# Layer-1 attention, near tiles: keeping the sums made for the maxima instead of making the product a second time

## The chip, the cores and the metric

The kernel runs on one core of a Trainium2 chip. The metric is the device time of one execution in microseconds, lower is better. Before the change the median of three runs is 1308.65 us (1305.66 to 1311.44).

## The reference

Two transformer-like layers over x of shape (2, 1024, 128). Each layer normalises x and adds to it an attention and a mixture-of-experts feed-forward block, both computed from the same normalised rows. Layer 0 has a causal sigmoid attention; layer 1 has a softmax attention with a relative position term, and only that one is touched here. Its core, for each of 16 heads of width 8:

```
q, k, v = heads(x @ Wq.T), heads(x @ Wk.T), heads(x @ Wv.T)
att_rel_pos = einsum('bhsd,pd->bhsp', q, pos_emb_k)           # pos_emb_k: 256 positions
att_idxs = clip(ar[None, :] - ar[:, None], -128, 127) % 256   # key index minus query index
att_pos = att_rel_pos[:, :, ar[:, None], att_idxs]
attn_val = einsum('bhqd,bhkd->bhqk', q, k)
att = softmax((attn_val + att_pos) / sqrt(8), axis=-1)
y = einsum('bhqk,bhkd->bhqd', att, v) ... @ Wproj.T
```

Because the index is clipped at 128, the position term of a pair of 128-row tiles varies from element to element only where query tile and key tile are the same or neighbours. Everywhere else it is one constant per query row.

## The kernel before, in words

The 1024 rows of a batch are 8 tiles of 128. Heads are handled four at a time: the 16 heads are split in four sets `s`, and in a set each of the four heads sits in its own group `r` of 32 partitions (`rows_of(r)`), so that TensorE can work on four heads side by side. A *group* `n` of work is one batch `b`, one set `s` and one half `q` of the queries (four query tiles, `i` = 0 to 3); there are 16 groups. Each group takes 8 *steps*, one for each key tile `kt`, so there are 128 steps `t`, with the key tile on the partitions and 512 queries along the columns.

For a group, in order of time:

- `by_position` makes the position scores of two query tiles at a time and writes them to a bounce buffer in HBM. `near_by` reads them back skewed, so that each query row is shifted by its own index. The result is the tile `near[n, i]`, of 128 queries x 4 heads x 384 columns: the position scores (less the far constant) of the three key tiles around query tile `i`. It lies in one of ten slots.
- `scan(n, i, half)` runs LEAD = 10 steps ahead of the step that uses it, one half of the keys each step. It makes the scores with the queries on the partitions (L902), and VectorE takes the row maxima: `tensor_reduce` (L927) where the position term is constant, and a sum-and-maximum (L922) where it isn't, which adds `near` to the scores, writes the sums to a scratch tile `junk`, and keeps only their maximum. After the second half L930 puts the negated maximum into a spare column of `negmax`.
- `augment` turns the negated maxima and adds them to the queries as an extra row of the contraction (`qa`), two steps ahead of the group's first step. So a product with `qa` comes out less the maximum. The far constants are in the keys in the same manner: `kls` for keys up to and with the near range, `khs` for keys above it.
- `scores(n, kt)` fills four PSUM banks, one for each head `r`. For query tiles near `kt` it turns the block of `near` into the bank (L953, with an identity), and then adds the product of keys and `qa` for all four query tiles to it (L963). ScalarE takes the exponential of each bank (L970).
- `values(n, kt, part)` multiplies the exponentials with the values (L982); it runs one step after its scores. `unload`, `finish` and `project` end a group or a half.

The banks come from one rotation of seven (`small()`). A step takes four for its scores and four for its scan, so that the fourth bank of the next step's scores is the first bank of this step's scan.

The order of TensorE's instructions is the program's order (`manual_schedule`); in each step it is: scores, values of the step before, scan, and then what stands beside. On the other engines a scheduler chooses the order of the instructions when the kernel is built; on the chip each engine then follows its own list. In the second batch GpSimd (POOL in the profile) also serves the mixture of experts: `gather(i)` fetches 128 rows by index (L630), and `gathered(i)` scales them (L640) and adds them to the result (L641). There are 64 of these, from step 68 on, placed three in four steps apart. `operands` makes `kls`, `khs` and `vs` on POOL too (L834, L837), once for each set, seven steps ahead of their first scan. Between step 66 and step 67 TensorE computes the experts (L704, L719). In the first batch POOL issues 64 scatters (L618), two each step from step 33 on, each held until the exponentials of its step (`paced`).

Of the kernel before, what the change touches and what calls it, by code (L numbers as in the profile page):

```python
# [10 lines left out]
F32 = mybir.dt.float32  # L11
AF = mybir.ActivationFunctionType
ALU = mybir.AluOpType
# [4 lines left out]
P = 128  # L18
# [3 lines left out]
NT = T // P  # L22
# [5 lines left out]
NG = 4  # L28
EPS = 1e-5
BIG = 3.0e38  # L30
# [11 lines left out]
NEAR = 3 * P  # L42
# [4 lines left out]
def fused_layers_kernel(ctx: ExitStack, tc: tile.TileContext, a: dict, out: bass.AP):  # L47
# [11 lines left out]
    nc = tc.nc  # L59
# [22 lines left out]
    def small():  # L82
        if "sm" not in psum:
            return big()[:, 0, :]
        return psum["sm"].tile([P, TB], F32, tag="sm", name="sm")
# [10 lines left out]
    def load(pool, name, shape, src=None):  # L96
        t = pool.tile(shape, F32, tag=name, name=name, bufs=1)
        nc.sync.dma_start(t, a[name] if src is None else src)
        return t
# [12 lines left out]
    w1 = load(l0, "w1", [P, E0 * I0])  # L112
# [656 lines left out]
    full, head, near, qa, negmax, yacc, probs = {}, {}, {}, {}, {}, {}, {}  # L769
# [23 lines left out]
    def four_banks():  # L793
        if "sm" in psum:
            return [small() for _ in range(NG)]
        pairs = [big(), big()]
        return [pairs[r // 2][:, r % 2, :] for r in range(NG)]

    def rows_of(r):
        return slice(32 * r, 32 * r + 32)  # L800
# [83 lines left out]
    def spans(lo, hi, cut):  # L884

        c = min(max(lo, cut), hi)
        return [(lo, c, 0)] * (lo < c) + [(c, hi, 1)] * (c < hi)
# [3 lines left out]
    def scan(n, i, half):  # L891

        b, s, q = groups[n]
        l1 = pools["l1"]
        qs, kl, kh, _ = head[b, s]
        qt = 4 * q + i
        ps = four_banks()
        lo, hi = 4 * half, 4 * half + 4
        for k0, k1, far in spans(lo, hi, qt + 2):
            for r in range(NG):  # L900
                g = rows_of(r)
                nc.tensor.matmul(  # L902
                    ps[r][:, (k0 - lo) * P:(k1 - lo) * P], qs[g, qt * P:(qt + 1) * P],
                    (kh if far else kl)[g, k0 * P:k1 * P], start=True, stop=True,
                )
        if half == 0:
            maxima[n, i] = l1.tile([P, NG, 4], F32, tag="maxima", name="maxima", bufs=3), []
        mx, used = maxima[n, i]
        n0, n1 = max(lo, qt - 1), min(hi, qt + 2)
        if n0 >= n1:  # L910
            pieces = [(lo, hi, False)]
        else:
            pieces = [(lo, n0, False)] * (lo < n0) + [(n0, n1, True)] + [(n1, hi, False)] * (n1 < hi)
        for k0, k1, close in pieces:
            slot = len(used)
            used.append(slot)
            for r in range(NG):
                part = ps[r][:, (k0 - lo) * P:(k1 - lo) * P]
                if close:
                    junk = l1.tile([P, NEAR], F32, tag="junk", name="junk")  # L920
                    w0 = (k0 - (qt - 1)) * P
                    nc.vector.tensor_tensor_reduce(  # L922
                        junk[:, 0:(k1 - k0) * P], part, near[n, i][:, r, w0:w0 + (k1 - k0) * P],
                        1.0, -BIG, ALU.add, ALU.max, mx[:, r, slot:slot + 1],
                    )
                else:
                    nc.vector.tensor_reduce(mx[:, r, slot:slot + 1], part, AX.X, ALU.max)  # L927
        if half == 1:
            out_ = negmax[s, i].rearrange("p (r c) -> p r c", r=NG)[:, :, aux[s]]
            nc.vector.tensor_reduce(out_, mx[:, :, 0:len(used)], AX.X, ALU.max, negate=True)  # L930

    def augment(n):

        b, s, q = groups[n]
        ps = small()
        for i in range(4):
            nc.tensor.matmul(
                ps[:, i * P:(i + 1) * P], negmax[s, i], ident, is_transpose=True, start=True, stop=True
            )
        t = pools["l1"].tile([P, TB], F32, tag="qa", name="qa", bufs=2)  # L940
        nc.vector.tensor_add(t, head[b, s][0][:, q * TB:(q + 1) * TB], ps)
        qa[n] = t

    def scores(n, kt):

        b, s, q = groups[n]
        _, kl, kh, _ = head[b, s]
        ps = [small() for _ in range(NG)]
        close = [i for i in range(4) if abs(4 * q + i - kt) <= 1]
        for r in range(NG):  # L950
            for i in close:
                w0 = (kt - (4 * q + i) + 1) * P
                nc.tensor.matmul(  # L953
                    ps[r][:, i * P:(i + 1) * P], near[n, i][:, r, w0:w0 + P], ident,
                    is_transpose=True, start=(i == close[0]), stop=False, skip_group_check=True,
                )

        cut = min(max(kt - 1 - 4 * q, 0), 4)
        parts = [(0, cut, kh)] * (cut > 0) + [(cut, 4, kl)] * (cut < 4)
        for m, (i0, i1, k) in enumerate(parts):  # L960
            for r in range(NG):
                g = rows_of(r)
                nc.tensor.matmul(  # L963
                    ps[r][:, i0 * P:i1 * P], k[g, kt * P:(kt + 1) * P], qa[n][g, i0 * P:i1 * P],
                    start=(m == 0 and not close), stop=(m == len(parts) - 1), skip_group_check=True,
                )
        p = pools["late"].tile([P, NG * TB], F32, tag="p", name="p", bufs=2)
        p = p.rearrange("p (r c) -> p r c", r=NG)
        for r in range(NG):
            e = nc.scalar.activation(p[:, r, :], ps[r], AF.Exp)  # L970
        last_exp["name"] = e.ins.name
        probs[n, kt] = p
# [129 lines left out]
    for m in range(LEAD):  # L1102
        at(N_ATT + 8 + m, scan, m // 8, m % 8 // 2, m % 2)
# [83 lines left out]
    with tc.manual_schedule(engines={mybir.EngineType.PE}):  # L1187
        near_by(1, 1)
        for t in range(N_STEPS + 1):
# [7 lines left out]
            if t < N_STEPS:  # L1197
                scores(t // 8, t % 8)


            n, kt = (t - 1) // 8, (t - 1) % 8
# [3 lines left out]
            m = t + LEAD  # L1205
            if m < N_STEPS:
                scan(m // 8, m % 8 // 2, m % 2)
# [9 lines left out]
            n, k = (t - 9) // 8, (t - 9) % 8  # L1217
            if t >= 9 and k == 0:
                unload(n)
            b, s, q = groups[min(max(n, 0), len(groups) - 1)]  # L1220
# [64 lines left out]
```

## Time and profile before

| | before |
|---|---|
| median of 3 runs | 1308.65 us |
| the profiled execution | 1308.08 us |
| its span | 1306.3 us |
| TensorE busy | 1197.7 us (92%) |
| VectorE busy | 759.4 us (58%) |
| ScalarE busy | 625.0 us (48%) |
| GpSimd busy | 378.2 us (29%) |
| steps of layer-1 attention, first batch | about 520 to 880 us |
| experts | about 880 to 1010 us |
| steps of layer-1 attention, second batch | about 1010 to 1306 us |

How to read it. The profile is of one execution. A row of the groups names a source line, the engine, the operation, what it writes and reads, and how often; then the busy time and the mean of one in ns; then how long the engine stood idle just before and who ended that. A matmul of fp32 operands is recorded as two, so the 704 transposes are 704 records, and the four products of a step eight. PEld is the loading of weights and overlaps PE. POOL's time that it stands waiting for a transfer isn't counted as busy. A timeline row has the start, the duration, the engine and the line, and in brackets the idle time of the engine ahead of it. Times that are not starts or durations of one instruction are in microseconds from the start of the span.

### The profile page before, as it was taken

What the parts mean: (1) busy time and instruction counts of PE and PEld (TensorE: products, weight loads), DVE (VectorE), ACT (ScalarE), POOL (GpSimd) and SP (SyncE); (2) the same over time, 40 slices, a digit from 0 to 9 for tenths busy, and PEclk for the clock granted to TensorE, in tenths of its full rate; (3) what the DMA queues carried; (4) which work ended last, traced back from release to release, by engine and by line L of the source; (5) the groups of instructions that cost most, each with busy time, mean ns of one, the idle gap of its engine ahead of it and who ended that gap; (6) DMA issues with size and microseconds to landing.
All of it is one profiled execution on the core that took longest, in us unless ns stands there. A gap on an engine that the chain in (4) does not pass through costs nothing.

```text
span 1306.3 us, 23125 instructions
## 1 busy us (share of the span) xinstructions
PE 1197.7 (92%) x8567; PEld 566.9 (43%) x8567; DVE 759.4 (58%) x2178; ACT 625.0 (48%) x1102; POOL 378.2 (29%) x464
## 2 busy tenths in 40 slices
PE   5889999989999878899799999988999999998997
PEld 2323332333333333434344354448999444443433
DVE  7783333573322358776876756764555856666653
ACT  3634444535455342454355654543444555554463
POOL 1123243323323242001002444330000445446453
PEclk9889999989999989899899999998999999998998
DMA  6682212111111261344365644659997354663511
GB/s 181 175 229 85 59 57 57 33 33 49 41 49 41 82 217 61 126 147 145 98 194 178 201 142 161 218 185 278 293 293 228 110 171 157 208 215 115 181 47 29
DMA packets 146660, 181.77 MB, mean 139 GB/s; under 512 B 16436, under 2 KB 125236, under 8 KB 146292
## 3 DMA queue, kind: packets, MB, share of 16 engines
q1 hardware_dynamic: 142292, 171.37, 42.7%
q0 software_dynamic: 4256, 8.92, 2.4%
q8 instruction: 68, 1.11, 0.4%
q14 instruction: 44, 0.36, 0.1%
HBM read 110.81 MB, written 73.77 MB: 141 GB/s over the span
## 4 chain that ended last, share of the span: by engine, by line
PE 70%; DVE 17%; DMA 5%; ACT 4%; issue 2%; POOL 1%; SPq 0%; DVEq 0%; ACTq 0%; POOLq 0%
PE sm L963 11%; PE sm L902 9%; PE acc L982 8%; PE big L340 6%; PE sm L953 5%; PE big L449 5%; PE big L341 5%; PE acc L475 5%; PE ffn L367 4%; PE sm L704 4%; DVE junk L922 3%; PE sm L853 3%; DVE maxima L927 2%; PE sm L719 2%; DMA room<-wx 1%
## 5 line engine op out<-in xcount | busy, mean ns | idle before, releaser
L970 ACT ACTIVATE p<-sm 128x512 f32<-128x512 f32 x512 | 264.7, 607 | 234.1 <-PE sm L963 233.6
L927 DVE TENSOR_REDUCE maxima<-sm 128x1 f32<-128x512 f32 (+3 forms) x472 | 226.7, 502 | 99.2 <-PE sm L902 99.2
L455 ACT ACTIVATE at<-big 128x1024 f32<-128x1024 f32 (+1 forms) x192 | 144.9, 808 | 149.7 <-PE big L449 143.7
L922 DVE CUSTOM_DVE_ANT_0 junk<-sm,near 128x384 f32<-128x384 f32 (+2 forms) x292 | 130.3, 446 | 66.3 <-PE sm L902 66.3
L982 PE MATMUL acc<-p,vs 128*32 128x512 f32 (+1 forms) x1288 | 146.4, 524 | 0.4 <-ACT yu L994 0.4
L352 DVE SCALAR_TENSOR_TENSOR t<-big,b,sg 128x512 f32<-128x512 f32 x64 | 47.9, 749 | 158.0 <-ACT sg L351 158.0
L355 POOL TENSOR_TENSOR h<-h,cb 128x512 f32<-128x512 f32 x64 | 82.8, 1294 | 195.5 <-DVE h L353 185.3
L953 PE MATMUL sm<-ident,near 128*128 128x128 f32 x704 | 108.4, 287 | 24.5 <-DVE maxima L927 11.3
L902 PE MATMUL sm<-kls,qs 32*128 32x512 f32 (+2 forms) x776 | 107.5, 580 | 6.2 <-POOL kls L834 5.0
L963 PE MATMUL sm<-qa,kls 32*128 32x512 f32 (+3 forms) x832 | 112.9, 560 | 0.0
L630 POOL DMA_INDIRECT got<-slots_y,slot_of x64 | 65.1, 1017 | 164.6 <-ACT p L970 152.5
L953 PEld LDWEIGHTS sm<-ident,near 128*128 128x128 f32 x704 | 78.0, 143 | 79.2 <-ACT p L970 35.4
L449 PE MATMUL big<-qm,xT 32*128 32x512 f32 (+3 forms) x768 | 103.8, 555 | 1.3 <-DVE xT L249 0.6
L618 POOL DMA_INDIRECT slots_x<-xn,slot_of x64 | 62.8, 981 | 95.8 <-ACT p L970 86.3
L475 PE MATMUL acc<-at,xn 128*32 128x512 f32 (+3 forms) x768 | 84.8, 514 | 5.9 <-POOL at L460 4.0
L340 PE MATMUL big<-xT,w 128*128 128x512 f32 x128 | 74.5, 665 | 14.9 <-DVE h L353 12.5
L857 ACT COPY rel<-sm 128x512 f32<-128x512 f32 x112 | 57.5, 600 | 61.6 <-PE sm L853 61.6
L640 POOL TENSOR_SCALAR got<-got,share 128x128 f32<-128x128 f32 x64 | 41.1, 642 | 110.1 <-DMA got<-slots_y,slot_of 110.0
L367 PE MATMUL ffn<-h,w 128*128 128x512 f32 x128 | 72.8, 651 | 0.0
L982 PEld LDWEIGHTS acc<-p,vs 128*32 128x32 f32 x1288 | 26.6, 109 | 105.9 <-issue 95.4
L902 PEld LDWEIGHTS sm<-kls,qs 32*128 32x128 f32 x776 | 36.9, 186 | 81.1 <-ACT p L970 21.1
L460 POOL TENSOR_SCALAR_AFFINE_SELECT at<-at 128x512 f32<-128x512 f32 x64 | 41.5, 648 | 101.6 <-ACT at L455 101.2
(285 smaller groups left out, 1659.8 us busy)
## 6 DMA issues: line engine op xcount, KB each, us to landing
bounce<-rel SPq DMA_DIRECT2D x64, 768.0 KB
near<-bounce SPq DMA_DIRECT2D x64, 768.0 KB
cb<-cw SPq DMA_DIRECT2D x128, 128.0 KB
blockw<-wx SPq DMA_DIRECT2D x53, 304.0 KB
room<-wx SPq DMA_DIRECT2D x26, 304.0 KB
slots_x<-zeros SPq DMA_DIRECT2D x19, 256.0 KB
slots_y<-by SPq DMA_DIRECT2D x19, 256.0 KB
room<-slots_x SPq DMA_DIRECT2D x17, 256.0 KB
```

Source lines behind the costliest of these rows:

```text
L340: nc.tensor.matmul(hh[0:m, 0, :], wa, xT, start=True, stop=True)
L367: nc.tensor.matmul(y, w2m, h[0:m], start=first, stop=last and bias_mm is None)
L449: nc.tensor.matmul(halves[r // 2][:, r % 2, off:TB], xT0[b][g, kt * P:(kt + 1) * P], masked[b, s][g, q * TB + off:(q + 1) * TB], start=Tru ...
L455: nc.scalar.activation(at[:, 2 * j:2 * j + 2, off:TB], sc[:, :, off:TB], AF.Sigmoid, scale=4.0 / math.sqrt(HD))
L475: nc.tensor.matmul(y[32 * r:32 * r + 32, off:TB], xn0[b][:, kt * P + 32 * r:kt * P + 32 * r + 32], at[:, r, off:TB], start=(kt == 0), stop ...
L902: nc.tensor.matmul(ps[r][:, (k0 - lo) * P:(k1 - lo) * P], qs[g, qt * P:(qt + 1) * P], (kh if far else kl)[g, k0 * P:k1 * P], start=True, s ...
L922: nc.vector.tensor_tensor_reduce(junk[:, 0:(k1 - k0) * P], part, near[n, i][:, r, w0:w0 + (k1 - k0) * P], 1.0, -BIG, ALU.add, ALU.max, mx[ ...
L927: nc.vector.tensor_reduce(mx[:, r, slot:slot + 1], part, AX.X, ALU.max)
L953: nc.tensor.matmul(ps[r][:, i * P:(i + 1) * P], near[n, i][:, r, w0:w0 + P], ident, is_transpose=True, start=(i == close[0]), stop=False, ...
L963: nc.tensor.matmul(ps[r][:, i0 * P:i1 * P], k[g, kt * P:(kt + 1) * P], qa[n][g, i0 * P:i1 * P], start=(m == 0 and not close), stop=(m == l ...
L970: e = nc.scalar.activation(p[:, r, :], ps[r], AF.Exp)
L982: nc.tensor.matmul(y[rows_of(r), part], vs[:, kt, rows_of(r)], probs[n, kt][:, r, part], start=(kt == 0), stop=(kt == NT - 1 and part.stop ...
```

## The change

The sums of scores and position scores that the scan makes for near tiles are kept in place, in `near` itself, and `junk` is gone. After the maximum of a query tile is known, its negation is added to the kept sums of the four heads: head 0 on ScalarE, head 1 on VectorE, heads 2 and 3 on GpSimd. The block that `scores` turns into the bank is then complete. The product with `qa` is left out for the near query tiles, and runs only over the query tiles ahead of them (with `khs`) and behind them (with `kls`). The loop over the transposes now has the query tile outside and the head inside, and each block is a group of its own in the bank.

```diff
                 if close:
-                    junk = l1.tile([P, NEAR], F32, tag="junk", name="junk")
+
                     w0 = (k0 - (qt - 1)) * P
+                    whole_ = near[n, i][:, r, w0:w0 + (k1 - k0) * P]
                     nc.vector.tensor_tensor_reduce(
-                        junk[:, 0:(k1 - k0) * P], part, near[n, i][:, r, w0:w0 + (k1 - k0) * P],
-                        1.0, -BIG, ALU.add, ALU.max, mx[:, r, slot:slot + 1],
+                        whole_, part, whole_, 1.0, -BIG, ALU.add, ALU.max, mx[:, r, slot:slot + 1],
                     )
...
             nc.vector.tensor_reduce(out_, mx[:, :, 0:len(used)], AX.X, ALU.max, negate=True)
+            w0, w1 = (max(qt - 1, 0) - (qt - 1)) * P, (min(qt + 2, NT) - (qt - 1)) * P
+            for r in range(NG):
+                t = near[n, i][:, r, w0:w1]
+                if r == 0:
+                    nc.scalar.activation(t, t, AF.Identity, bias=out_[:, r:r + 1])
+                else:
+                    (nc.vector if r == 1 else nc.gpsimd).tensor_scalar(t, t, out_[:, r:r + 1], None, ALU.add)
...
-        close = [i for i in range(4) if abs(4 * q + i - kt) <= 1]
-        for r in range(NG):
-            for i in close:
-                w0 = (kt - (4 * q + i) + 1) * P
+        c0, c1 = (min(max(kt + d - 4 * q, 0), 4) for d in (-1, 2))
+        for i in range(c0, c1):
+            w0 = (kt - (4 * q + i) + 1) * P
+            for r in range(NG):
                 nc.tensor.matmul(
                     ps[r][:, i * P:(i + 1) * P], near[n, i][:, r, w0:w0 + P], ident,
-                    is_transpose=True, start=(i == close[0]), stop=False, skip_group_check=True,
+                    is_transpose=True, start=True, stop=True,
                 )
-        cut = min(max(kt - 1 - 4 * q, 0), 4)
-        parts = [(0, cut, kh)] * (cut > 0) + [(cut, 4, kl)] * (cut < 4)
-        for m, (i0, i1, k) in enumerate(parts):
+        for i0, i1, k in ((0, c0, kh), (c1, 4, kl)):
             for r in range(NG):
-                g = rows_of(r)
-                nc.tensor.matmul(
-                    ps[r][:, i0 * P:i1 * P], k[g, kt * P:(kt + 1) * P], qa[n][g, i0 * P:i1 * P],
-                    start=(m == 0 and not close), stop=(m == len(parts) - 1), skip_group_check=True,
-                )
+                if i0 < i1:
+                    g = rows_of(r)
+                    nc.tensor.matmul(
+                        ps[r][:, i0 * P:i1 * P], k[g, kt * P:(kt + 1) * P], qa[n][g, i0 * P:i1 * P],
+                        start=True, stop=True,
+                    )
```

In the profile of the changed kernel the sum-and-maximum is L923, the subtraction on ScalarE is L935, those on VectorE and GpSimd are L937, the transposes are L960, the products L969 and the exponentials L976; L927, L930 and the gathers' L630, L640 and L641 keep their numbers.

## The prediction

> **What bounds the kernel now.** I read first the page's busy shares and its chain, then TensorE's timeline over one near group, then POOL's timeline over the last third, and last what the tile of the gathered rows waits for.
>
> ```profile
> PE 1197.7 (92%) x8567; PEld 566.9 (43%) x8567; DVE 759.4 (58%) x2178; ACT 625.0 (48%) x1102; POOL 378.2 (29%) x464
> PE 70%; DVE 17%; DMA 5%; ACT 4%; issue 2%; POOL 1%; SPq 0%; DVEq 0%; ACTq 0%; POOLq 0%
> L953 PE MATMUL sm<-ident,near 128*128 128x128 f32 x704 | 108.4, 287 | 24.5 <-DVE maxima L927 11.3
> L963 PE MATMUL sm<-qa,kls 32*128 32x512 f32 (+3 forms) x832 | 112.9, 560 | 0.0
> ```
>
> TensorE is bound on average, and POOL at 29% looks free. Averages hide stages, so next TensorE's timeline in attention of layer 1 (start, duration, engine, line, form, count, idle before):
>
> ```profile
> 668.95 1.14 PE L902 MATMUL sm<-kls,qs 32*128 32x512 f32 x8
> 670.02 0.55 PE L953 MATMUL sm<-ident,near 128*128 128x128 f32 x3
> 671.02 0.30 PE L953 MATMUL sm<-ident,near 128*128 128x128 f32 x1 [0.45 <-DVE maxima L922]
> 671.25 1.14 PE L963 MATMUL sm<-qa,kls 32*128 32x512 f32 x8
> ...
> 674.39 1.27 PE L953 MATMUL sm<-ident,near 128*128 128x128 f32 x8
> 675.59 1.14 PE L963 MATMUL sm<-qa,kls 32*128 32x512 f32 x8
> 676.66 1.07 PE L982 MATMUL acc<-p,vs 128*32 128x512 f32 x8
> ...
> 678.73 1.53 PE L953 MATMUL sm<-ident,near 128*128 128x128 f32 x12
> 680.19 1.14 PE L963 MATMUL sm<-qa,kls 32*128 32x512 f32 x8
> ```
>
> Twelve transposes take 1.46 us start to start, 0.122 each; a full product L963 takes 1.07, so 0.268 per 128 columns. The fourth head group (r=3) cannot start until DVE has emptied a bank of the scan before it: with four transposes TensorE stops after three and resumes 1.00 us after it began. With twelve, r=3 comes after nine and nothing stops.
>
> Now POOL near the end, with TensorE's line at the same time:
>
> ```profile
> 1179.97 1.01 POOL L630 DMA_INDIRECT got<-slots_y,slot_of  x1 [0.15 <-issue]
> 1182.67 0.60 POOL L640 TENSOR_SCALAR got<-got,share 128x128 f32<-128x128 f32 x1 [1.68 <-DMA got<-slots_y,slot_of]
> 1183.35 0.45 POOL L641 TENSOR_TENSOR x<-x,got 128x128 f32<-128x128 f32 x1
> 1183.80 1.19 POOL L834 TENSOR_SCALAR khs<-kf,not_aux,k_add 128x1024 f32<-128x1024 f32 x1
> 1184.98 1.19 POOL L834 TENSOR_SCALAR kls<-kf,not_aux,k_add 128x1024 f32<-128x1024 f32 x1
> 1186.22 1.45 PE L902 MATMUL sm<-kls,qs 32*128 32x256 f32 x8 [5.03 <-POOL kls L834]
> 1294.86 0.61 POOL L641 TENSOR_TENSOR x<-x,got 128x128 f32<-128x128 f32 x1
> ```
>
> This is the reading that matters. POOL issues a gather, waits for it, scales it, adds it, then issues the next. All 64 run from 1020.25 to 1295.47: 275.2 us, 4.30 each, of which only 136.3 are busy and 110.0 are waits for the DMA. They are placed at 0.75 step each; a step of TensorE here is about 4.4 us, so it allows 3.3. POOL is busy half the time and yet **late**, by more each step: keys placed seven steps ahead already cost TensorE 5 us at 1186. Nothing else urgent stood in that queue.
>
> **What the Trainium skill says.** "PSUM — Partial Sum Buffer", Engine vs sequencer instructions: the queues of ScalarE, VectorE and GpSimd are strictly first in, first out. The trace agrees: the key operands at 1183.80 sat behind the gathers. "DMA: Bandwidth & Descriptors", Anatomy of one DMA: a transfer issued by GpSimd has a fixed cost of about 2 us, mostly the receipt; here the median from issue to landing is 2.7. "GPSIMD Engine Reference", Elementwise: 512 elements of one input took 769 ns; this trace's 128x512 select (L460) took 648 and I use the trace. "SBUF — State Buffer", Who interferes with whom: a VectorE instruction in a two-port mode blocks GpSimd wholly. L640 has 0.60 us as median and 1.30 as maximum, so blocking may be there; I use it for the upper price only.
>
> **The change part by part.**
>
> Removed: the second product for near blocks. Of 32 blocks (8 key tiles x 4 query tiles) in a group 11 are near; 16 x 11 x 0.268 = 47 us of TensorE, if nothing else came up. The transposes stay, 704.
>
> Moved: the transposes now run with r innermost, so r=3 is always fourth. By the 1.00 us above, twelve take 1.00 + 9 x 0.122 = 2.10 (was 1.46), eight 1.61 (was 1.20), four stay 1.23. Two groups (q=0 and 1) have 4, 4 and 2 such steps: 4 x 0.64 + 4 x 0.41 = 4.2 us back of 11 x 2 x 0.268 = 5.9. The compiled order of DVE also changes: for the second query tile, four sums L923 now come ahead of the four other reductions. That frees the first bank 3 x 0.47 = 1.4 us later, once ahead of a twelve-transpose step and once ahead of a step without near blocks. Net for two groups -1.7 + 1.4 to 2.8, so between -0.3 and +1.1. For the 8 groups ahead of the gathers -1 to +4; with a good day for the overlaps -15, with ACT's waits below +8. I take **0**.
>
> The sum kept instead of junk: same instruction, same size, same engine; the write goes to SBUF as before. Nothing, and no transfer is delayed, since a near slot is refilled only after its transposes anyway.
>
> Added on DVE: 64 subtractions of up to 384 columns. L234 (128 columns) 0.34, L824 (1024) 0.79: about 0.47, one in two steps. DVE idles over 1 us in a near step (58% busy); hidden, else 64 x 0.47 = 30 us. On ACT: 64 of 384 columns, 0.48 as the 384-column copies L696; ACT idles 1.4 to 2.9 us a step. It stands among the exponentials and waits for the maximum; behind it are two or three exponentials that free banks and feed L982. That is in the +8.
>
> Added on POOL: 128 subtractions, r=2 and 3. Not in the trace as such. L640 has 0.60 at 128 columns, L834 1.19 at 1024: 0.66 ns a column, so 0.77 at 384 and 0.68 at 256, plus 0.08 between instructions. A quarter have 256 columns: 0.83 each. Flat bound 0.68; upper bound 1.08 (blocked by VectorE, or the slope of a two-input add). Below nothing is excluded: the work is new. Until the gathers POOL waits for exponentials of the same step, and the tiles are needed five steps or more later: hidden. In the compiled queue 25 pairs stand among the gathers, each between one row's addition and the next gather, so the DMA waits do not cover them; the last two pairs stand behind all 64 gathers. Queued behind them: all later gathers. Waiting for them: TensorE's transposes, five to twelve steps after the scan. SP's queue gains nothing.
>
> Sum, for the last group's tile i=2, needed in step 125:
> - first gather 1020.3 + 0; gathers 275.2; 50 subtractions x 0.83 = 41.4; fewer waits for the DMA, as the same near and bounce traffic spreads over 15% more time: waits above their floor of 57 (each four gathers: 0.3 + 1.63 + 1.63) are 53, of which 13% is 7. POOL ends at 1329.9.
> - tail: step 125's third tile started at 1281.3 of 1306.3, so 25.0 remain, less 2.1 for narrower products, less 1.4 as the very last pair is needed later: 21.5. Span 1351.4.
> - plus 1308.1 - 1306.3 = 1.8: **1353 us**, against the profiled execution's 1308.1, +45; the median of the runs, 1308.65, is 0.6 higher, within my rounding.
>
> TensorE first stops at step 82: tile i=3 of group 10 stands behind 14 gathers and seven pairs (60 + 13 us) and is wanted after 14 x 4.4 = 62. From there it follows POOL.
>
> **The rivals.** *POOL keeps up (faster).* If TensorE stayed the bound, the result is 1308 less 8 x 1.7 = 14: about 1294. For it: 110 us of POOL's stage are waits. Against: even at no price the subtractions behind the gathers are ready at 1295, and step 125 wants them at 1281. The stage must shrink by 14 + 41 = 55 us, more than all 53 of avoidable waits. *Only TensorE's new stalls.* If POOL were somehow in time, but the bank waits and ACT's place in the queue cost the upper figure: 1308 + 8 x 1.1 = 1317. It decides if r=3's bank is freed later than 1.7 us after the transposes begin. *Worse than the sum.* POOL blocked by VectorE at 1.08 each, the waits not fewer, and the groups ahead of the gathers at +8: 1353 + 13 + 7 + 8 = 1381; beyond, if each stop of TensorE also lowers its granted clock (0.87 in the stretch with the 5 us stop).
>
> **How the numbers follow.** POOL's queue 0.83; POOL in time 0.08, of which most faster; only the stalls 0.04; worse 0.05. The unknowns of the first give 1353 - 7 (flat price) - 13 (more of the waits gone) - 15 = 1318, and 1381 upward. Range 1318 to 1381, about 8 in 10. A measurement of this kernel can tell about 0.5%, 6.5 us, from no change. Faster 0.07, same 0.04, slower 0.89.
>
> **What would show it.** Right: the transposes (L960 then) waiting tens of us for POOL's subtraction (L937) after 1080; POOL's last instruction a subtraction near 1330, about 21 us ahead of the end; the products (L969) shorter by some 40 us busy; TensorE idle from about 1080 on, little change at 1020. Wrong: gathers under 3.5 us each, POOL ending by 1285, the transposes waiting mostly for ACT or DVE, or the first gather moved by over 15 us.

## The result, and the profile after

The changed kernel takes 1418.96 us, median of 4 runs (1400.51 to 1421.84), against 1309.36 us for the kernel before, median of 4 runs. The ratio is 1.0793, 95% interval 1.0686 to 1.0901. (The ratio compares the means of the fast runs: the run at 1421.84, over 1.5% above the fastest, counts as slow and is left out, so it isn't the quotient of the medians.) The profiled execution took 1416.86 us, its span 1415.1 us: 63.7 us more than the 1351.4 of the prediction's sum.

The page of the changed kernel, first the same rows as before: busy shares, the chain, the transposes and the largest row of the products; then the two new rows of subtractions, on ScalarE and GpSimd.

```profile
PE 1238.5 (88%) x8247; PEld 573.3 (41%) x8247; DVE 782.3 (55%) x2242; ACT 656.5 (46%) x1166; POOL 536.4 (38%) x592
PE 54%; DVE 20%; DMA 10%; ACT 6%; POOL 5%; issue 5%; SPq 0%; DVEq 0%; ACTq 0%; POOLq 0%
L937 POOL TENSOR_SCALAR near<-near,negmax 128x384 f32<-128x384 f32 (+1 forms) x128 | 156.7, 1232 | 307.8 <-DVE negmax L930 235.1
L960 PE MATMUL sm<-ident,near 128*128 128x128 f32 x704 | 125.2, 308 | 69.9 <-POOL near L937 38.9
L935 ACT ACTIVATE near<-near,negmax 128x384 f32<-128x384 f32 (+1 forms) x64 | 37.7, 589 | 168.0 <-DVE negmax L930 109.8
L969 PE MATMUL sm<-qa,kls 32*128 32x512 f32 (+3 forms) x512 | 84.1, 524 | 4.9 <-DVE maxima L927 3.2
```

TensorE's share of the chain fell from 70% to 54%; DMA, POOL, VectorE, ScalarE and issue took it. TensorE issues 320 records less and yet is recorded as busy for longer: a longer busy time doesn't mean more work here (the last section has the lower granted clock of this run). The row to look at is L937: 1.232 us for one, where the prediction's sum had 0.77 and 0.68 for the two sizes. Kept apart by shape it reads:

```profile
L937 POOL TENSOR_SCALAR near<-near,negmax 128x384 f32<-128x384 f32 x96 | 126.4, 1325 | 268.1 <-DVE negmax L930 210.2 <-issue 26.4 <-DVE chosen L274 17.3
L937 POOL TENSOR_SCALAR near<-near,negmax 128x256 f32<-128x256 f32 x32 | 30.3, 954 | 39.7 <-DVE negmax L930 24.9 <-issue 14.8
```

The waits of the changed kernel from 500 us to the end (who <- for whom: us in total, times, longest):

```profile
POOL got L640 <- DMA got<-slots_y,slot_of: 108.8, 49, 6.7
ACT near L935 <- DVE negmax L930: 106.0, 34, 6.7
PEld sm L960 <- POOL near L937: 43.4, 15, 13.1
PE sm L960 <- POOL near L937: 38.9, 12, 12.9
```

The last two rows are the same stops seen by the weight loads and by the matmuls, so TensorE stood some 40 us for POOL's subtraction. The first row is the DMA wait of the gathers, 108.8 against 110.0 before: the gathers wait as they did. And ScalarE stood in front of its own subtraction for 106 us. Whether these waits of ScalarE cost anything is a question for the experiments.

POOL's timeline towards the end, and TensorE's at the same time:

```profile
1335.11 1.02 POOL L630 DMA_INDIRECT got<-slots_y,slot_of  x1 [0.15 <-issue]
...
1340.47 2.47 POOL L937 TENSOR_SCALAR near<-near,negmax 128x384 f32<-128x384 f32 x2
1343.11 1.04 POOL L630 DMA_INDIRECT got<-slots_y,slot_of  x1 [0.16 <-issue]
1345.76 0.61 POOL L640 TENSOR_SCALAR got<-got,share 128x128 f32<-128x128 f32 x1 [1.62 <-DMA got<-slots_y,slot_of]
...
1387.42 4.28 POOL L937 TENSOR_SCALAR near<-near,negmax 128x384 f32<-128x384 f32 x4
```

```profile
1336.43 1.83 PE L960 MATMUL sm<-ident,near 128*128 128x128 f32 x10
1341.78 0.48 PE L960 MATMUL sm<-ident,near 128*128 128x128 f32 x1 [3.51 <-POOL near L937]
1343.00 0.48 PE L960 MATMUL sm<-ident,near 128*128 128x128 f32 x1 [0.75 <-POOL near L937]
```

Ten of twelve transposes run, then heads 2 and 3 wait until POOL has made their subtractions at 1340.47, and those stand between an addition and the next gather. The last two pairs, at 1387.42, stand behind all 64 gathers. Since POOL's last instruction ends at 1391.70, the span divides into three parts:

| us | prediction's sum | measured | more |
|---|---|---|---|
| start to first gather | 1020.3 | 1059.1 | 38.8 |
| first gather to end of POOL | 309.6 | 332.6 | 23.0 |
| end of POOL to end | 21.5 | 23.4 | 1.9 |

More than half of what was missed lies ahead of the gathers, where POOL's subtractions were taken to be hidden and the rest to cost 0. There the layer-1 steps of the first batch, from the first near transpose to the experts' first instruction, take 397.8 us against 362.7 before; 4.0 of the 38.8 lie ahead of that stretch and the experts are 0.3 shorter. One place in it, read on three engines: ScalarE, then TensorE, then the one instruction of VectorE that both wait for.

```profile
649.06 2.06 ACT L976 ACTIVATE p<-sm 128x512 f32<-128x512 f32 x4 [2.16 <-PE sm L969]
655.11 0.61 ACT L935 ACTIVATE near<-near,negmax 128x384 f32<-128x384 f32 x1 [3.98 <-DVE negmax L930]
655.63 2.04 ACT L976 ACTIVATE p<-sm 128x512 f32<-128x512 f32 x4
```

```profile
651.09 0.55 PE L960 MATMUL sm<-ident,near 128*128 128x128 f32 x3
652.92 0.30 PE L960 MATMUL sm<-ident,near 128*128 128x128 f32 x1 [1.28 <-DVE maxima L923]
653.15 0.93 PE L969 MATMUL sm<-qa,khs 32*128 32x384 f32 x8
654.58 1.46 PE L902 MATMUL sm<-kls,qs 32*128 32x512 f32 x6
656.26 1.12 PE L902 MATMUL sm<-kls,qs 32*128 32x512 f32 x2 [0.22 <-ACT p L976]
```

```profile
654.90 0.17 DVE L930 TENSOR_REDUCE negmax<-maxima 128x4 f32<-128x12 f32 x1
```

ScalarE is done with four exponentials at 651.12 and stands 3.98 us in front of its subtraction, whose maximum VectorE makes in the instruction at 654.90. The next four exponentials are behind it in the queue, although TensorE's products for them are under way from 653.15. They start at 655.63, and the scan's last matmuls (656.26) wait for a bank that the first of them empties. The same lines show the other stop: the fourth transpose waits 1.28 us for a bank that VectorE empties.

### The profile page after: what moved, and what is told of

It reads as the page before. It is cut to its first block, busy times and chain, and to the rows that moved or that the text cites. A ratio compares the mean times of both kernels' runs of the same rounds, so it can differ in the third digit from the quotient of the medians.

```text
span 1415.1 us, 22799 instructions
## 1 busy us (share of the span) xinstructions
PE 1238.5 (88%) x8247; PEld 573.3 (41%) x8247; DVE 782.3 (55%) x2242; ACT 656.5 (46%) x1166; POOL 536.4 (38%) x592
## 3 DMA queue, kind: packets, MB, share of 16 engines
q1 hardware_dynamic: 142292, 171.37, 38.8%
## 4 chain that ended last, share of the span: by engine, by line
PE 54%; DVE 20%; DMA 10%; ACT 6%; POOL 5%; issue 5%; SPq 0%; DVEq 0%; ACTq 0%; POOLq 0%
PE sm L902 7%; PE acc L988 6%; DMA got<-slots_y,slot_of 6%; DVE maxima L927 5%; PE big L340 5%; PE sm L969 5%; PE sm L960 4%; PE big L449 4%; PE acc L475 4%; PE big L341 4%; DVE near L923 4%; PE sm L704 4%; PE ffn L367 4%; ACT p L976 2%; POOL near L937 2%
## 5 line engine op out<-in xcount | busy, mean ns | idle before, releaser
L976 ACT ACTIVATE p<-sm 128x512 f32<-128x512 f32 x512 | 265.3, 601 | 194.4 <-PE sm L969 193.8
L927 DVE TENSOR_REDUCE maxima<-sm 128x1 f32<-128x512 f32 (+3 forms) x472 | 220.8, 501 | 118.9 <-PE sm L902 112.5
L937 POOL TENSOR_SCALAR near<-near,negmax 128x384 f32<-128x384 f32 (+1 forms) x128 | 156.7, 1232 | 307.8 <-DVE negmax L930 235.1
L960 PE MATMUL sm<-ident,near 128*128 128x128 f32 x704 | 125.2, 308 | 69.9 <-POOL near L937 38.9
L923 DVE CUSTOM_DVE_ANT_0 near<-sm,near 128x384 f32<-128x384 f32 (+2 forms) x292 | 124.8, 446 | 77.5 <-PE sm L902 76.5
L988 PE MATMUL acc<-p,vs 128*32 128x512 f32 (+1 forms) x1288 | 158.0, 562 | 0.6 <-ACT yu L1000 0.6
L902 PE MATMUL sm<-kls,qs 32*128 32x512 f32 (+2 forms) x776 | 143.1, 630 | 8.4 <-ACT p L976 8.3
L960 PEld LDWEIGHTS sm<-ident,near 128*128 128x128 f32 x704 | 87.4, 153 | 138.5 <-POOL near L937 43.4
L935 ACT ACTIVATE near<-near,negmax 128x384 f32<-128x384 f32 (+1 forms) x64 | 37.7, 589 | 168.0 <-DVE negmax L930 109.8
L902 PEld LDWEIGHTS sm<-kls,qs 32*128 32x128 f32 x776 | 48.6, 202 | 110.7 <-ACT p L976 50.9
L969 PE MATMUL sm<-qa,kls 32*128 32x512 f32 (+3 forms) x512 | 84.1, 524 | 4.9 <-DVE maxima L927 3.2
L640 POOL TENSOR_SCALAR got<-got,share 128x128 f32<-128x128 f32 x64 | 40.6, 634 | 109.3 <-DMA got<-slots_y,slot_of 108.8
L853 PE MATMUL sm<-posd,qs 32*128 32x256 f32 x448 | 61.8, 434 | 17.1 <-DVE maxima L927 15.1
```

What stands on the lines that cost most here:

```text
L902: nc.tensor.matmul(ps[r][:, (k0 - lo) * P:(k1 - lo) * P], qs[g, qt * P:(qt + 1) * P], (kh if far else kl)[g, k0 * P:k1 * P], start=True, s ...
L923: nc.vector.tensor_tensor_reduce(whole_, part, whole_, 1.0, -BIG, ALU.add, ALU.max, mx[:, r, slot:slot + 1],)
L937: (nc.vector if r == 1 else nc.gpsimd).tensor_scalar(t, t, out_[:, r:r + 1], None, ALU.add)
L960: nc.tensor.matmul(ps[r][:, i * P:(i + 1) * P], near[n, i][:, r, w0:w0 + P], ident, is_transpose=True, start=True, stop=True,)
L969: nc.tensor.matmul(ps[r][:, i0 * P:i1 * P], k[g, kt * P:(kt + 1) * P], qa[n][g, i0 * P:i1 * P], start=True, stop=True,)
L988: nc.tensor.matmul(y[rows_of(r), part], vs[:, kt, rows_of(r)], probs[n, kt][:, r, part], start=(kt == 0), stop=(kt == NT - 1 and part.stop ...
```

## The experiments

Each started from the changed kernel unless the text says otherwise. "First batch" is from the first near transpose to the experts' first instruction, "gather stage" from the first gather to the end of POOL's last instruction, both in the one profiled execution. The same kernel profiled twice (e10 and e13) differs by 0.2 and 0.5 us in these two; the times of the changed kernel's four runs lie 21 us apart. Each ratio compares means with runs of the kernel before that were made beside that experiment (medians 1305.4 to 1306.2 us), not with the first row.

| | median us | ratio to before, 95% | first batch | gather stage |
|---|---|---|---|---|
| before | 1309.36 | | 362.7 | 275.2 |
| changed | 1418.96 | 1.0793 (1.0686 to 1.0901) | 397.8 | 332.6 |
| e1 no subtraction on POOL | 1361.94 | 1.0420 (1.0364 to 1.0476) | 391.0 | 276.7 |
| e2 transposes: head outside | 1403.46 | 1.0738 (1.0707 to 1.0769) | 387.1 | 327.8 |
| e3 no subtraction on ScalarE | 1379.74 | 1.0557 (1.0526 to 1.0587) | 367.2 | 326.9 |
| e4 other form on POOL | 1386.19 | 1.0606 (1.0524 to 1.0687) | 399.7 | 293.6 |
| e5 no subtraction | 1307.38 | 1.0012 (0.9999 to 1.0024) | 366.9 | 271.0 |
| e6 before, head inside | 1322.0 | 1.0119 (1.0065 to 1.0172) | 376.0 | 268.2 |
| e8 scan: head outside | 1388.62 | 1.0641 (1.0596 to 1.0686) | 378.1 | 319.7 |
| e9 all on VectorE, both orders | 1297.77 | 0.9941 (0.9920 to 0.9963) | 351.4 | 272.9 |
| e10 paced, two on ScalarE | 1282.97 | 0.9820 (0.9791 to 0.9849) | 344.5 | 267.1 |
| e11 only ScalarE's paced | 1380.77 | 1.0581 (1.0538 to 1.0623) | 374.8 | 321.6 |
| e12 paced, four on ScalarE | 1281.0 | 0.9810 (0.9783 to 0.9837) | 344.4 | 268.6 |
| e13 as e10, again | 1279.14 | 0.9808 (0.9783 to 0.9833) | 344.3 | 267.6 |

**e1, the subtractions of heads 2 and 3 on VectorE.**

```diff
-                    (nc.vector if r == 1 else nc.gpsimd).tensor_scalar(t, t, out_[:, r:r + 1], None, ALU.add)
+                    (nc.vector).tensor_scalar(t, t, out_[:, r:r + 1], None, ALU.add)
```

> The subtractions of heads 2 and 3 move from POOL to VectorE (three there, one on ScalarE); all else as in the changed kernel. Theory 'POOL's queue': only the part after the first gather was bound by POOL. That part took 356 us in the changed kernel and 286 before; without POOL's work it should run like the first batch, which lost about 35 us to other waits, so about 286 + 35 = 320, and the total about 1380; gathers take about 275 us again, the transposes wait for POOL not at all, and the first gather stays near 1059. Rival 'same loss in both halves, POOL only follows': the second half stays near 356 and the total near 1417. If VectorE is the tight engine, the first gather moves later than 1059 by up to 27 us (two more subtractions of 0.42 us in each of 32 query tiles).

The gather stage is back at 276.7 us. TensorE's longest waits from 1050 us to the end of e1 begin so, and POOL's subtraction is in none of the rows:

```profile
PE sm L960 <- DVE maxima L927: 10.0, 16, 1.8
PE sm L853 <- DVE maxima L927: 4.3, 5, 1.8
```

The queue of POOL is confirmed as the cost of the gather stage, which loses 55.9 us; the span loses 57.5, and the total came 18 us under what I expected. But 51 us over before are left. The first batch explains about 28 of them (391.0 against 362.7). Behind the end of POOL there are now 27.4 us (1330.2 to 1357.6) instead of the 10.8 of before: it looks as if what slows the first batch slows the second one too, and in the changed kernel lay hidden behind POOL. Why the first batch is 6.8 us shorter here is open, since e4 finds POOL's price hidden there.

**e2, the transposes with the head outside and the query tile inside, as before the change.**

```diff
-        for i in range(c0, c1):
-            w0 = (kt - (4 * q + i) + 1) * P
-            for r in range(NG):
+        for r in range(NG):
+            for i in range(c0, c1):
+                w0 = (kt - (4 * q + i) + 1) * P
```

> Only the loop over the transposes is put back: head outside, query tile inside, so that the fourth head comes last again. Theory 'bank wait' for the 35 us lost ahead of the experts: up to 4.2 us come back in two groups, 17 in four pairs, so the first gather moves from 1059 to about 1042 and the total to about 1400. Rival 'ScalarE waits in its queue': nothing of that kind changes, first gather within 5 us of 1059, total within 7 us of 1417.

The first batch is 10.7 us shorter, not the 17 that four times 4.2 would be. The bank wait is there, at about two thirds of the size.

**e3, head 0's subtraction on VectorE, none on ScalarE.**

```diff
-                if r == 0:
-                    nc.scalar.activation(t, t, AF.Identity, bias=out_[:, r:r + 1])
-                else:
-                    (nc.vector if r == 1 else nc.gpsimd).tensor_scalar(t, t, out_[:, r:r + 1], None, ALU.add)
+                (nc.vector if r < 2 else nc.gpsimd).tensor_scalar(t, t, out_[:, r:r + 1], None, ALU.add)
```

> The subtraction of head 0 moves from ScalarE to VectorE (two there, two on POOL), so that no instruction of ScalarE waits for a maximum between exponentials. Theory 'ScalarE waits in its queue': TensorE's waits for exponentials at the scan (L902), 37 us in the steps of the first batch against 16 before, go back to about 16, and the first gather comes at about 1038; the end moves as much or more, total about 1395. Rival 'bank wait' or 'VectorE': first gather at 1059 or later, total 1417 or more.

The first batch falls from 397.8 to 367.2, the largest single effect there. It doesn't say yet whether ScalarE's work costs that or its waiting; e11 does.

**e4, POOL's subtraction written as a multiplication by one and an addition.** The same tiles, in the same place of the queue; only the form of the instruction is another.

```diff
-                    (nc.vector if r == 1 else nc.gpsimd).tensor_scalar(t, t, out_[:, r:r + 1], None, ALU.add)
+                    nc.gpsimd.tensor_scalar(t, t, 1.0, out_[:, r:r + 1], ALU.mult, ALU.add)
```

> POOL's subtraction is written as times 1.0 plus the negated maximum, the two-operation form that L834 has, in place of a single add; same result, same tile. In the changed kernel one takes 1.33 us at 384 columns and 0.95 at 256, and L640, a single multiply, 0.60 at 128: a straight line of 2.6 to 3 ns a column; L834 has 1.19 at 1024 columns. Theory 'the form sets the price': about 0.6 us at 384 columns, 50 x 0.65 = 33 us less in the stage of the gathers, total about 1385. Rival 'working in place, or blocking by VectorE, sets the price': 1.2 to 1.3 us stay, total 1417.

POOL's groups of e4, by shape:

```profile
L939 POOL TENSOR_SCALAR near<-near,negmax 128x384 f32<-128x384 f32 x96 | 62.6, 659 | 282.1 <-DVE negmax L930 219.5 <-issue 27.8 <-DVE chosen L274 18.7
L939 POOL TENSOR_SCALAR near<-near,negmax 128x256 f32<-128x256 f32 x32 | 16.5, 522 | 43.8 <-DVE negmax L930 27.2 <-issue 16.5
```

More arithmetic in half the time: 1.325 to 0.659 us at 384 columns, 0.954 to 0.522 at 256. The gather stage loses 39.0 us, and TensorE's waits for POOL are down to

```profile
PEld sm L962 <- POOL near L939: 8.0, 6, 6.0
PE sm L962 <- POOL near L939: 6.5, 4, 5.6
```

The first batch is no shorter (399.7): there POOL's price is indeed hidden, as predicted. A blocking of POOL by VectorE, the prediction's reason for its upper price, doesn't explain the price, since the same tiles in the same places of the queue cost half.

**e5, all four subtractions left out.**

```diff
-            for r in range(NG):
-                t = near[n, i][:, r, w0:w1]
-                if r == 0:
...
-                    (nc.vector if r == 1 else nc.gpsimd).tensor_scalar(t, t, out_[:, r:r + 1], None, ALU.add)
...
-            e = nc.scalar.activation(p[:, r, :], ps[r], AF.Exp)
+            e = nc.scalar.activation(p[:, r, :], ps[r], AF.Exp, scale=1e-3)
```

> Leaves out all four subtractions (the near blocks keep their maximum, and the exponentials take a scale of 0.001 so that they stay finite); kept sums, narrower products, loop order and VectorE's order stay as in the changed kernel. It is the bound of what better placed subtractions can reach with the rest unchanged. Theory 'ScalarE in the first batch, POOL in the second': first-batch steps as without ScalarE's part or a little less, about 360 us to the experts (367 there, 398 changed, 363 before), and the second half like before, about 286: total about 1300. If the 47 us of product were free to take, it would be 1265. Rival 'the kept sums or the loop order cost as much as the subtractions': total above 1340.

This is the most telling miss of mine. With the second product gone and no subtraction in its place the kernel is as fast as before, 1.0012. So the other edits take back what the product saves, and two are left to suspect: the order of the transposes (e2, e6) and the order of VectorE's work (e8). Those runs price them one by one in other kernels; this kernel with both orders put back was not run. The scale in the exponential only keeps its results finite.

**e6, the kernel before with the transposes' loop turned, and nothing else.**

```diff
-        for r in range(NG):
-            for i in close:
+        for i in close:
+            for r in range(NG):
```

> The kernel before, with one edit: in the transposes the query tile is the outer loop and the head the inner one, as in the changed kernel. Theory 'bank wait': putting the order back in the changed kernel gave 10.7 us in the first batch (398 to 387), so here 10 us are lost in each batch, total about 1328. My prediction's figure of 4.2 us in two groups would give 34, total 1342. Rival 'the order matters only with VectorE's new order': within 5 us of 1308.

The loop alone costs 13.3 us in the first batch and 1.2% in all. It is a cost of the order and not of the changed kernel's other waits.

**e8, the scan's maxima with the head outside and the piece inside.** The scratch tile `junk` had one buffer, so in the kernel before each head's sum had to be done with before the next head's could be written; VectorE took sums and reductions in turn. In the changed kernel the scheduler puts four sums first in nine scans ahead of the experts, and in eight more, of 256 columns, three sums in a row behind one sum and one reduction. That the lost buffer is the reason is read from the program; no run changes it alone. This edit writes the old order into the program.

```diff
-        for k0, k1, close in pieces:
-            slot = len(used)
-            used.append(slot)
-            for r in range(NG):
+        first = len(used)
+        used.extend(range(first, first + len(pieces)))
+        for r in range(NG):
+            for slot, (k0, k1, close) in enumerate(pieces, first):
```

> The changed kernel with one edit: in the scan the head is the outer loop and the piece the inner one, so that VectorE takes sum and reduction head by head again, as it did while all sums shared the scratch tile. Theory 'the lost scratch tile put the four sums first and frees the first bank late', by my sizes 1.4 to 2.8 us in two groups: 6 to 11 us back in the first batch, 398 to about 390, total about 1405. Rival 'hidden behind ScalarE's waits': within 4 us of 398, total 1415.

VectorE's timeline over one scan, in the kernel before (the sum is L922), in the changed kernel and in e8 (L927 reduces and is a bank's other user; the bank is free when both have run):

```profile
670.11 0.29 DVE L927 TENSOR_REDUCE maxima<-sm 128x1 f32<-128x128 f32 x1 [1.41 <-PE sm L902]
670.32 0.55 DVE L922 CUSTOM_DVE_ANT_0 junk<-sm,near 128x384 f32<-128x384 f32 x1
...
670.79 0.29 DVE L927 TENSOR_REDUCE maxima<-sm 128x1 f32<-128x128 f32 x1
670.99 0.55 DVE L922 CUSTOM_DVE_ANT_0 junk<-sm,near 128x384 f32<-128x384 f32 x1
```

```profile
676.01 0.56 DVE L923 CUSTOM_DVE_ANT_0 near<-sm,near 128x384 f32<-128x384 f32 x1 [1.70 <-PE sm L902]
...
677.92 0.88 DVE L927 TENSOR_REDUCE maxima<-sm 128x1 f32<-128x128 f32 x4
```

```profile
675.89 0.29 DVE L927 TENSOR_REDUCE maxima<-sm 128x1 f32<-128x128 f32 x1 [2.17 <-PE sm L902]
676.10 0.55 DVE L923 CUSTOM_DVE_ANT_0 near<-sm,near 128x384 f32<-128x384 f32 x1
...
676.57 0.28 DVE L927 TENSOR_REDUCE maxima<-sm 128x1 f32<-128x128 f32 x1
676.77 0.55 DVE L923 CUSTOM_DVE_ANT_0 near<-sm,near 128x384 f32<-128x384 f32 x1
```

The first bank is free about 2.2 us after VectorE begins in the changed kernel, and about 0.8 in e8. The first batch falls by 19.7 us. The lag of 1.4 us was read rightly in the prediction; what it costs was not.

**e9, all subtractions on VectorE, with the orders of e2 and e8.** No diff of its own: `nc.vector.tensor_scalar(t, t, out_[:, r:r + 1], None, ALU.add)` for all heads, and the two loops above.

> The changed kernel with all four subtractions on VectorE, the transposes with the head outside, and the scan's maxima with the head outside, so that VectorE again takes sum and reduction head by head. Theory 'queues of ScalarE and POOL, and bank wait': all three losses are gone; VectorE has 4 x 0.42 = 1.7 us more in two steps, of which it idles about 2.5. First-batch steps about 355 us, second half about 280, total about 1290 to 1310. Rival 'VectorE becomes the bound': transposes and scans wait for maxima, up to 64 x 1.3 = 80 us more than before would be the worst, total above 1320.

A gain of 0.6%; the interval leaves out 1. (The 14 runs lie between 1290.9 and 1305.4, and the profiled one, 1292.0, is among the fastest.) From the changed kernel to here the first batch loses 46.4 us, more than the 35.1 that the change had added. The three single undoings add up to 61.0 (30.6, 10.7, 19.7), or 53.4 with e11's value in place of e3's: either they overlap, one stop covering another, or VectorE's three more subtractions cost something. The runs don't tell.

**e11, only ScalarE's subtraction later.** It is issued one scan later, and placed behind the last exponential of that step in ScalarE's queue (`paced`). The work on ScalarE is the same as in the changed kernel.

```diff
                 if r == 0:
-                    nc.scalar.activation(t, t, AF.Identity, bias=out_[:, r:r + 1])
+                    pending.append((t, out_[:, r:r + 1]))
...
+        else:
+            subtract()
...
+    def subtract():
+        while pending:
+            t, bias = pending.pop(0)
+            d = nc.scalar.activation(t, t, AF.Identity, bias=bias)
+            if last_exp:
+                paced(d)
```

> The changed kernel with one edit: ScalarE's subtraction is issued one step later and held until the last exponential of that step, so that its maximum is known when it comes up; its work, POOL's and VectorE's subtractions, the loop orders stay. Theory 'ScalarE lost time by waiting in its queue': the same gain as without any subtraction on ScalarE, first-batch steps about 367 to 372 us (398 in the changed kernel, 367 without ScalarE's), first gather at about 1030, total about 1385. Rival 'by the work': 398 stay, total 1417.

The first batch falls from 397.8 to 374.8. TensorE's waits of the scan for exponentials in that stretch, first the changed kernel, then e3, then e11:

```profile
PEld sm L902 <- ACT p L976: 32.8, 35, 2.0
```

```profile
PEld sm L902 <- ACT p L973: 16.7, 19, 2.0
```

```profile
PEld sm L902 <- ACT p L988: 16.9, 18, 2.1
```

Taking ScalarE's subtraction away and only moving it bring this wait to the same value, 19 and 18 times instead of 35. So most of e3's gain, 23.0 of 30.6, is the waiting in the queue, not ScalarE's work. The other 7.6 are not told apart: in e3 VectorE has the work.

**e10, e12, e13: all of it together.** The orders of e2 and e8; the subtractions one scan later as in e11, for heads 0 and 1 on ScalarE and heads 2 and 3 on VectorE (e10, and the same again as e13), or all four on ScalarE (e12). The part for e10 and e13 that shares the heads out; e12 has `r < 4`:

```diff
...
-                if r == 0:
-                    nc.scalar.activation(t, t, AF.Identity, bias=out_[:, r:r + 1])
+                if r < 2:
+                    d = nc.scalar.activation(t, t, AF.Identity, bias=out_[:, r:r + 1])
+                    if last_exp:
+                        paced(d)
                 else:
-                    (nc.vector if r == 1 else nc.gpsimd).tensor_scalar(t, t, out_[:, r:r + 1], None, ALU.add)
+                    nc.vector.tensor_scalar(t, t, out_[:, r:r + 1], None, ALU.add)
```

> As the one with all on VectorE, but heads 0 and 1 on ScalarE and 2 and 3 on VectorE, and all subtractions placed one step later, ScalarE's held until the last exponential of that step, so that their maximum is long known. Theory 'ScalarE lost time only by waiting in its queue, not by the work': 2 x 0.6 us in two steps fit in its idle time, the scan's wait for exponentials falls to the 16 us of before, first-batch steps about 350 us, total about 1280 to 1295, ahead of all on VectorE by 5 to 15. Rival 'the work itself delays the exponentials': slower than all on VectorE.

> As the one with two subtractions paced on ScalarE, but all four there. ScalarE's work in two steps grows to 4 x 0.56 = 2.2 us beside 4.1 of exponentials and 1.0 of position copies, 7.3 of about 8.3; VectorE is freed of 0.9. Theory 'VectorE's lateness in freeing banks is what is left': faster than 1283 by up to 10. Rival 'ScalarE gets tight and the exponentials come late': slower than 1283, about 1295.

> The kernel with two subtractions paced on ScalarE and two on VectorE once more, for its interval: 1283 within 5, ratio 0.980 to 0.985.

These beat both kernels: 0.9808 (0.9783 to 0.9833) for e13, and e12 can't be told from it. ScalarE's and TensorE's timelines of e13 over a step with three near tiles:

```profile
675.62 2.06 ACT L988 ACTIVATE p<-sm 128x512 f32<-128x512 f32 x4 [1.85 <-PE sm L981]
677.72 1.12 ACT L945 ACTIVATE near<-near,negmax 128x384 f32<-128x384 f32 x2
679.58 2.06 ACT L988 ACTIVATE p<-sm 128x512 f32<-128x512 f32 x4 [0.74 <-PE sm L981]
```

```profile
677.60 1.53 PE L972 MATMUL sm<-ident,near 128*128 128x128 f32 x12
679.06 0.50 PE L981 MATMUL sm<-qa,kls 32*128 32x128 f32 x8
679.49 1.07 PE L1000 MATMUL acc<-p,vs 128*32 128x512 f32 x8
```

The subtractions stand right behind four exponentials, with no wait ahead of them, and are done before the next products arrive; twelve transposes run without a stop, and the product is 0.50 us for the one far tile, where the kernel before had 1.14 us for four (671.25, in the prediction's lines).

## Why the prediction was wrong in size, point by point

The direction was right, and so was the mechanism that was to set the end: POOL's queue of gathers, made longer by the subtractions. The sum was 63.7 us short, and these are the terms of it.

**"First gather 1020.3 + 0".** This step failed most, by 38.8 us, 35.1 of them in the steps of the first batch: it put the sum of gain and stalls at nothing. Three parts of it were named, but each was sized from one reading and netted against the product saved. (a) *ACT's waits, "in the +8".* They cost 23.0 us in the first batch by e11, 30.6 by e3. The prediction named what stands behind the subtraction, two or three exponentials, and didn't price how long they stand: ScalarE's idle 1.4 to 2.9 us a step was counted as room for 0.48 us of work, while the question was when the maximum comes. The Trainium skill's "PSUM — Partial Sum Buffer", Engine vs sequencer instructions, says that ScalarE's queue is strictly first in, first out; I quoted it and drew a price from it for POOL alone. The trace agrees here too, with the 3.98 us at 655.11. (b) *VectorE's order, 1.4 to 2.8 us for two groups*, so 6 to 11 for the first batch: e8 showed 19.7. It was counted at one or two steps of two groups, and the changed kernel's nine scans with four sums first are about as many; nine lags of 1.4 are 12.6. The rest of the 19.7 may be the eight scans in which the later banks come late, which the prediction didn't count; no run keeps the two apart. (c) *The loop order, 4.2 us for two groups*, so 17: 10.7 by e2 and 13.3 by e6, a little too high. The product saved was sized somewhat too high: TensorE is busy with products (L963, L981) for 166.0 us in the kernel before and 128.8 in e13, 37 less, where the sum had 47; in the changed kernel itself (L969) it is 145.8. As an estimate, 23.0, 19.7 and 10.7 less half of the 37 come to 35, the loss that was measured; since the parts may overlap, some of that agreement is luck. And the granted clock is another rival: it was 0.92 in the first batch, against 0.96 before. Scaling TensorE's 355 us of busy time there by the two, an estimate, makes up to 15 of the 35 us the clock's; no run tells whether the stops lowered it.

**"50 POOL subtractions x 0.83 = 41.4".** The count was right: POOL has 252 instructions in the gather stage against 202 before. The price was not: 1.325 and 0.954 us instead of 0.77 and 0.68. POOL's busy time there rises by 58.8 (204.1 against 145.3), and the stage by 57.4. The step that failed is the slope: I drew one line through L640 (128 columns, 0.60 us) and L834 (1024 columns, 1.19 us), which are two forms, a multiplication alone and a multiplication with an addition. By e4 the two follow different lines, and the changed kernel used the dear one. The upper price of 1.08 was meant to hold the term and was too low as well.

**"Fewer waits for the DMA, 7".** They were 108.8 us against 110.0: 1 instead of 7. Price (58.8 busy instead of the 37.4 that 0.77 and 0.68 give) and waits together, about 21 + 6, give 27 where 23.0 was missed.

**The tail, 21.5.** Measured 23.4, and POOL's last instruction is a subtraction, as predicted. Around the span 1.8, as predicted.

**"TensorE first stops at step 82" (about 1082).** Wrong. Seven pairs at 0.83 are 11.6 us, not 13, but that decides little. With the first gather 39 us later it should have come at about 1121; the trace has the first stop for POOL at 1205. Why the lag grew that slowly was not tried.

**The rivals.** *POOL keeps up* asked for the stage to shrink by 55 us and gave 1294; e9 and e13 take POOL out of it in another way and come to 1298 and 1279. That is near, but both also put back the two orders, which this rival kept, so it confirms little. *Only the stalls*, at 1317, was far too cheap: e1, which has the stalls without POOL (and two more subtractions on VectorE), took 1362. *Worse than the sum* had the right signs for the price and for the groups ahead of the gathers, and stopped at 1381 because its two worst prices were 1.08 and +8.

**The signs.** Of those for being right, the waits of the transposes for POOL's subtraction (38.9 us) came, and POOL's last instruction, a subtraction, 23.4 us ahead of the end; the products are 20 us shorter in the changed kernel, not 40. Of those for being wrong one came: the first gather moved by over 15 us.

**What stays open.** e13 gains 29 us of span where TensorE's products are 37 us shorter. The scan's matmuls L902 are recorded as 10 us longer in it (171.0 against 160.6), which no run explains. Its POOL ends at 1272.6 of 1277.1, so the gathers may be next in line.

## What to carry to other kernels

Work moved to a lightly loaded engine is priced by its place in that engine's queue: ask when its input comes and what stands behind it, and if the input is late, issue it later, as e11 did without removing any work. Price an instruction only from rows of its own form. And before you count a removed operation as a gain, list the orders that its buffers and loops had imposed: here VectorE's old order and a loop order were worth as much as the product that was removed (19.7 and 10.7 us in the first batch by e8 and e2; e5 for the whole).

## What the runs showed of the hardware

**One operation costs POOL twice what two do.** With a per-row operand, fp32, in place, the addition alone took 0.954 us at 256 columns and 1.325 at 384, about 2.9 ns a column; the multiplication and addition in one instruction took 0.522 and 0.659, about 1.1 ns a column. The Trainium skill's "GPSIMD Engine Reference", Elementwise, which the prediction drew on, gives 769 ns for 512 elements as its best case, 1.5 ns each. The first form took 1325 ns for 384, 3.5 each, well above that; the second took 659, 1.7 each, and as L834 1190 for 1024 columns, 1.2 each, below it. The measurement decides.

**The granted clock was lower where TensorE kept stopping.** Two stretches of the changed kernel (start and end, length, busy time of PE, PEld, DVE, ACT, POOL, then the granted clock, DMA share and GB/s):

```profile
1320.00:1392.00 72.00, 52.18 (x374) 20.83 (x375) 25.49 (x67) 29.34 (x58) 48.87 (x60) 0.79 0.12 35
1260.00:1320.00 60.00, 52.96 (x426) 23.32 (x425) 39.00 (x131) 31.74 (x62) 34.79 (x43) 1.00 0.46 146
```

Where it waited for POOL, by up to 12.9 us at a time, the granted clock was 0.79; in the 60 us ahead of that, without such waits, 1.00. The transposes after a wait for POOL at 1341.78 and 1343.00 took 0.48 us each, the one at 652.92, after a wait of 1.28 us, 0.30. Over the whole run the clock was 0.932 against 0.966 before; in the gather stage 0.88 against 0.98. A stop thus seems to cost more than its own length; no run separates the two.
